# Loading eight 128 x 128 matrices in long runs and sorting their rows on the chip, in a kernel that streams 128 products

## The chip, the cores and the metric

The kernel runs on one core of a Trainium2 chip. The metric is the device time of one execution in microseconds (us); smaller is better. The kernel before takes 323.64 us (median of three runs, 323.44 to 323.72). Engines have short names in the profile: PE (TensorE), DVE (VectorE), ACT (ScalarE), POOL (GpSimd), SP (SyncE). ScalarE and SyncE each issue DMA transfers into a queue of their own; the transfers of both run on the core's 16 DMA engines.

## The reference

All of it is in float32. `x` holds 128 matrices of 128 x 1024, `weights` eight matrices of 128 x 128, and `itok_B_0_7` names for each x one of the eight (0 to 7). What is computed is x plus the product with the chosen matrix:

```
w = weights[subjects]                        # (128, 128, 128): b, c, d
out = x + einsum('bct,bcd->bdt', x, w)       # (128, 128, 1024)
```

x and the output are 67.1 MB each, the eight matrices 0.52 MB.

## The kernel before

The work goes in 32 turns of four x (`H * G` = 4, `NT` = 32), each turn in two halves of two. The x of a turn live in one of 12 slots of `x_all` (16 KB in each partition); turn i uses slot i mod 12. A slot is loaded, its products are added in place, and it is stored from the same place.

Each engine has its own list of work, written out by hand in one critical section; semaphores tie the lists together:

- **ScalarE** only issues loads (lines 200 to 204): four for a turn, each of one x (512 KB) by `transfer` (line 59), with the DRAM side written as 32 runs of 16 KB (`ROWS` = 4 rows of x in a run). The first 12 turns wait for nothing; from turn 12 on it waits until the slot's last store has landed (`s_slot`, line 202).
- **SyncE** issues the subjects (line 180) and then the matrices (line 181). The matrices go to `w_all[c, s, d]`, partition c: with `weights.rearrange("s c d -> c s d")` each contiguous run is one row of 128 elements, 512 B, so there are 1024 runs. Then it waits until slot 7 has been loaded (line 213, `AHEAD` = 8), and from there it stores turn after turn, each as soon as its additions are counted in `s_added` (lines 214 to 218; the last turn in halves, the very last x by line 238).
- **GpSimd** only waits for the loads of each turn and then raises `s_ready` (lines 206 to 211).
- **VectorE** clears a tile for PE's idle products (line 183), puts the subjects in order (193 to 199), waits for the matrices (line 222), copies the first four chosen matrices to `ws` (`place`, line 153) and then loops over the turns: for each half it adds the product from PSUM to x in place (`add`, line 174) and copies the next turn's two matrices.
- **TensorE** runs three idle products on zeros (line 186), then loops over the turns: for each half it waits for `s_go` (matrices in `ws`) and `s_ready` (x loaded), and does four products of 128 x 128 by 128 x 512 (line 162).

So the order of the transfers is set by two lists: loads in ScalarE's, stores in SyncE's. Whatever stands ahead of a load in ScalarE's list delays that load and all behind it.

Of the kernel before, what the change touches and what calls it, by code (L numbers as in the profile page):

```python
# [30 lines left out]
G = 2  # L31
H = 2
# [3 lines left out]
SLOTS = 12  # L36
# [5 lines left out]
DMA = 16  # L42

IDLE = 3

ROWS = 4

ALIGN = 4096
QUEUES = {mybir.EngineType.SP: "qSPDynamicHW", mybir.EngineType.Activation: "qActDynamicHW"}
# [2 lines left out]
def transfer(nc, engine, out, in_):  # L52

    later, nc._always_lower_symbolic_ap = nc._always_lower_symbolic_ap, False
    ins, outs = engine.lower_ap_dma(in_), engine.lower_ap_dma(out)
    nc._always_lower_symbolic_ap = later
    return engine.add_instruction(
        mybir.InstDMACopy(  # L60
            name=nc.get_next_instruction_name(),
            engine=engine.engine,
            ins=ins,
            outs=outs,
            mode="Copy",
            cce_op=ALU.bypass,
            queue=QUEUES[engine.engine],
        )
    )
# [3 lines left out]
def kernel(  # L73
# [7 lines left out]
    nc = tc.nc  # L81
    B, C, T = x.shape
    S, _, D = weights.shape
    NT = B // (G * H)

    def sbuf(name, *shape, dtype=F32):
        return ctx.enter_context(nc.sbuf_tensor(name, list(shape), dtype)).ap()
# [5 lines left out]
    x_all = sbuf("x_all", C, SLOTS * H * G * T)  # L93
# [1 line left out]
        x_all[:, i * H * G * T : (i + 1) * H * G * T].rearrange("c (q t) -> c q t", t=T)  # L95
        for i in range(SLOTS)
    ]
    w_all = sbuf("w_all", C, S, D)
    ws = [sbuf(f"w{i}", C, 1, D) for i in range(H * G)]
    zeros = sbuf("zeros", C, N)  # L100
    given, near, wrap = (sbuf(name, 1, B, dtype=I32) for name in ("given", "near", "wrap"))
# [3 lines left out]
    ]  # L105

    s_given = tc.alloc_semaphore("s_given")
    s_wall = tc.alloc_semaphore("s_wall")
    s_index = tc.alloc_semaphore("s_index")
    s_zeros = tc.alloc_semaphore("s_zeros")  # L110
# [9 lines left out]
    def emptied(i):  # L120
        turns = i // SLOTS
        return DMA * (H * G + 1) * turns - (DMA * G if i >= SLOTS and i % SLOTS == 0 else 0)

    def load(engine, i, q):
        transfer(
            nc,
            engine,
            xs[i % SLOTS][:, q, :],
            x[i * H * G + q].rearrange("(a r) t -> a (r t)", r=ROWS),
        ).then_inc(s_head if i * H * G + q < G else s_slot[i % SLOTS], DMA)  # L130

    def store(i, q0, q1):
        b = i * H * G
        transfer(
            nc,
            nc.sync,
            out[b + q0 : b + q1].rearrange("g d t -> d g t"),
            xs[i % SLOTS][:, q0:q1, :].rearrange("d (o g) t -> d o (g t)", g=min(G, q1 - q0)),
        ).then_inc(s_slot[i % SLOTS], DMA)

    def subjects_of(i):
        _, subject = nc.values_load_multi_w_load_instructions(
            index[0:1, i] if isinstance(i, slice) else index[0:1, bass.ds(i * (H * G), H * G)],
            engines=[mybir.EngineType.DVE],
            min_val=0,
            max_val=S - 1,
            skip_runtime_bounds_check_because="the index is clamped on the chip above",
        )
        return subject

    def place(h, subject):
        for q in range(h * G, (h + 1) * G):
            copy = nc.vector.tensor_copy(ws[q], w_all[:, bass.ds(subject[q], 1), :])  # L153
        copy.then_inc(s_go, 1)

    def multiply(slot, h):
        nc.tensor.wait_ge(s_go, 1).then_inc(s_go, -1)
        nc.tensor.wait_ge(s_ready, 1).then_inc(s_ready, -1)  # L158
        for q in range(h * G, (h + 1) * G):
            for t in range(0, T, N):  # L160
                at = slot * (H * G * T) + (q * T + t)
                mm = nc.tensor.matmul(  # L162
                    ps[h][:, q % G, t : t + N],
                    ws[q][:, 0, :],
                    x_all[:, bass.ds(at, N)],
                    start=True,
                    stop=True,
                )
        mm.then_inc(s_product, 1)

    def add(slot, h):
        mine = x_all[:, bass.ds(slot * (H * G * T) + h * G * T, G * T)]
        nc.vector.wait_ge(s_product, 1).then_inc(s_product, -1)  # L173
        nc.vector.tensor_tensor(  # L174
            mine, ps[h].rearrange("d g t -> d (g t)"), mine, ALU.add
        ).then_inc(s_added, 1)

    with tc.tile_critical():  # L178

        nc.sync.dma_start(given, subjects.rearrange("(o b) -> o b", o=1)).then_inc(s_given, DMA)  # L180
        nc.sync.dma_start(w_all, weights.rearrange("s c d -> c s d")).then_inc(s_wall, DMA)

        nc.vector.memset(zeros, 0.0).then_inc(s_zeros, 1)  # L183
        nc.tensor.wait_ge(s_zeros, 1)
        for _ in range(IDLE):
            nc.tensor.matmul(  # L186
                ps[P_SLOTS - 1][:, G - 1, :N], zeros[:, :D], zeros, start=True, stop=True
            )

        nc.vector.memset(index[:, B:], 0).then_inc(s_index, 1)  # L193
        nc.vector.wait_ge(s_given, DMA)
        nc.vector.tensor_scalar(near, given, -S, S - 1, ALU.max, ALU.min).then_inc(s_index, 1)  # L195
        nc.vector.wait_ge(s_index, 2)
        nc.vector.tensor_scalar(wrap, near, 0, S, ALU.is_lt, ALU.mult).then_inc(s_index, 1)  # L197
        nc.vector.wait_ge(s_index, 3)
        nc.vector.tensor_tensor(index[:, :B], near, wrap, ALU.add).then_inc(s_index, 1)  # L199
        for i in range(NT):  # L200
            if i >= SLOTS:
                nc.scalar.wait_ge(s_slot[i % SLOTS], emptied(i))
            for q in range(H * G):
                load(nc.scalar, i, q)

        for i in range(NT):
            if i == 0:
                nc.gpsimd.wait_ge(s_head, DMA * G).then_inc(s_ready, 1)
                nc.gpsimd.wait_ge(s_slot[0], DMA * G).then_inc(s_ready, 1)
            else:  # L210
                nc.gpsimd.wait_ge(s_slot[i % SLOTS], emptied(i) + DMA * H * G).then_inc(s_ready, H)

        nc.sync.wait_ge(s_slot[AHEAD - 1], DMA * H * G)
        for i in range(NT):
            for h in range(H):
                if i == NT - 1 or h == H - 1:
                    nc.sync.wait_ge(s_added, i * H + h + 1)
                    store(i, h * G if i == NT - 1 else 0, (h + 1) * G - (i * H + h == NT * H - 1))


        nc.vector.wait_ge(s_index, 4)
        nc.vector.wait_ge(s_wall, DMA)
        subject = subjects_of(slice(0, H * G))
        for h in range(H):
            place(h, subject)
        with nc.vector.Fori(0, NT) as turn:  # L226
            subject = subjects_of(turn + 1)
            for h in range(H):
                add(turn % SLOTS, h)
                place(h, subject)  # L230
        with nc.tensor.Fori(0, NT) as turn:
            for h in range(H):
                multiply(turn % SLOTS, h)
# [39 lines left out]
```

## Time and profile before

| | us |
|---|---|
| median of three runs (lowest, highest) | 323.64 (323.44, 323.72) |
| the profiled execution | 323.44 |
| its span, first to last instruction | 321.7 |
| PE busy | 244.1 |
| DVE busy | 165.7 |
| POOL busy | 0.2 |

The span is what the trace covers; the rest of the execution's time, 1.74 us, lies around it. ScalarE has no row of busy time, since it only issues transfers, which do not count as busy.

How to read the lines that the prediction quotes. A page divides the span into 40 equal slices; in the row `DMA` each digit is the mean busy share of the 16 DMA engines in tenths, in `GB/s` what they moved. A queue's line has its packets, its MB and the time of its packets as a share of 16 engines' time. A line of the view by stretches begins with the stretch (from:to, us), then its length, then each engine's busy time and instructions (PE, PE's weight loads, DVE, POOL), then the granted PE clock, the share of the DMA engines (packets overlap a little, so it can pass 1) and GB/s. A line of a group has busy time in us, mean ns of one, and the idle time before the group with what ended it. A line of the timeline begins with start and length in us. `ACTq` and `SPq` are the transfers' issues on ScalarE's and SyncE's lists; in a view of one line they have least, median and longest issue in ns, and the first and the last start.

### The profile page before, as it was taken

Reading aid. Unit: us, or ns where it says so; the run is one execution under the profiler, and the core shown is the slowest. Engines: PE = TensorE matmul, PEld = TensorE weight load, DVE = VectorE, ACT = ScalarE, POOL = GpSimd, SP = SyncE. Lnnn points to the kernel's source line nnn. Section 1 sums busy time; section 2 is a strip of 40 time slices with the busy share of each in tenths; the row PEclk is TensorE's granted clock in tenths of the full one; section 3 lists DMA queues with packets and bytes.
Section 4 is the critical chain, followed back from the end, with each engine's and each line's share of the span. In section 5 each row is a group of like instructions: output and inputs, shape, how many; then the busy total and the mean of one; then the engine's idle time right before and its main releaser. Section 6 shows DMA issues by size and latency. Waiting matters only on the chain. (4 is left out here: it accounts for less than half of the span.)

```text
span 321.7 us, 2380 instructions
## 1 busy us (share of the span) xinstructions
PE 244.1 (76%) x518; PEld 101.0 (31%) x518; DVE 165.7 (52%) x202; POOL 0.2 (0%) x4
## 2 busy tenths in 40 slices
PE   5999999999999999959499684986959779300000
PEld 2434444443444444424143231432423234000000
DVE  2267776777677677736627465371754707500000
POOL 0000000000000000000000000000000000000000
PEclk9799999999999999979879999897998959755555
DMA  7999999999999999999999999999999999999997
GB/s 281 426 428 426 424 424 408 421 437 418 421 438 428 422 418 426 439 427 423 424 418 425 434 435 413 426 433 427 428 418 425 440 417 421 426 430 425 427 428 309
DMA packets 16051, 134.76 MB, mean 419 GB/s; under 512 B 2609, under 2 KB 3634, under 8 KB 3890
## 3 DMA queue, kind: packets, MB, share of 16 engines
q1 hardware_dynamic: 9906, 67.64, 50.1%
q10 hardware_dynamic: 6144, 67.12, 49.6%
q14 instruction: 1, 0.01, 0.0%
HBM read 67.63 MB, written 67.11 MB: 419 GB/s over the span
## 5 line engine op out<-in xcount | busy, mean ns | idle before, releaser
L162 PE MATMUL ps<-x_all,w 128*128 x512 | 239.6, 626 | 30.2 <-PEq L158 27.1
L174 DVE TENSOR_TENSOR x_all<-ps,x_all 128x2048 f32 x64 | 146.7, 2292 | 106.9 <-DVEq L173 106.9
L162 PEld LDWEIGHTS ps<-x_all,w 128*128 128x128 f32 x512 | 99.3, 199 | 170.5 <-issue 169.7
L153 DVE COPY w<-w_all 128x128 f32 x132 | 23.2, 219 | 4.3 <-DMA w_all<-in_L_cond_weights_dram 4.3
L186 PE MATMUL ps<-zeros 128*128 128x512 f32 x6 | 4.4, 897 | 1.7 <-DVE zeros L183 1.7
L186 PEld LDWEIGHTS ps<-zeros 128*128 128x128 f32 x6 | 1.7, 304 | 3.6 <-issue 1.9
L183 DVE MEMSET zeros<- 128x512 f32 x1 | 0.5, 485 | 1.0 <-SPq L178 1.0
L195 DVE TENSOR_SCALAR near<-given 1x128 int32<-1x128 int32 x1 | 0.2, 217 | 0.6 <-DMA given<-in_itok_B_dram 0.6
L199 DVE CUSTOM_DVE_ANT_0 index<-near,wrap 1x256 uint16<-1x256 uint16 x1 | 0.3, 280 | 0.0
L197 DVE TENSOR_SCALAR wrap<-near 1x128 int32<-1x128 int32 x1 | 0.2, 215 | 0.0
L260 POOL MEMSET const-bfloat16-1.0<- 128x1 bf16 x1 | 0.1, 101 | 0.0
L260 POOL MEMSET const-uint8-127<- 128x1 uint8 x1 | 0.1, 101 | 0.0
L260 POOL MEMSET const-float32-0.0<- 128x1 f32 x1 | 0.1, 98 | 0.2 <-issue 0.2
L260 POOL MEMSET const-float32-1.0<- 128x1 f32 x1 | 0.1, 98 | 0.0
L260 DVE BASE_LOAD x1 | 0.0, 21 | 0.1
L193 DVE MEMSET index<- 1x4 int32 x1 | 0.1, 62 | 0.0
## 6 DMA issues: line engine op xcount, KB each, us to landing
x_all<-in_x_dram ACTq DMA_DIRECT2D x128, 512.0 KB, 10.7
out_dram<-x_all SPq DMA_DIRECT2D x31, 2048.0 KB, 54.8
out_dram<-x_all SPq DMA_DIRECT2D x1, 1024.0 KB, 26.0
out_dram<-x_all SPq DMA_DIRECT2D x2, 512.0 KB, 21.0
w_all<-in_L_cond_weights_dram SPq DMA_DIRECT2D x1, 512.0 KB, 5.1
given<-in_itok_B_dram SPq DMA_DIRECT2D x1, 0.5 KB
```

The costliest lines, as they stand in the source:

```text
L153: copy = nc.vector.tensor_copy(ws[q], w_all[:, bass.ds(subject[q], 1), :])
L162: mm = nc.tensor.matmul(ps[h][:, q % G, t : t + N], ws[q][:, 0, :], x_all[:, bass.ds(at, N)], start=True, stop=True,)
L174: nc.vector.tensor_tensor(mine, ps[h].rearrange("d g t -> d (g t)"), mine, ALU.add).then_inc(s_added, 1)
L183: nc.vector.memset(zeros, 0.0).then_inc(s_zeros, 1)
L186: nc.tensor.matmul(ps[P_SLOTS - 1][:, G - 1, :N], zeros[:, :D], zeros, start=True, stop=True)
L193: nc.vector.memset(index[:, B:], 0).then_inc(s_index, 1)
L195: nc.vector.tensor_scalar(near, given, -S, S - 1, ALU.max, ALU.min).then_inc(s_index, 1)
L197: nc.vector.tensor_scalar(wrap, near, 0, S, ALU.is_lt, ALU.mult).then_inc(s_index, 1)
L199: nc.vector.tensor_tensor(index[:, :B], near, wrap, ALU.add).then_inc(s_index, 1)
L260: nc = _bacc.Bacc("TRN2", target_bir_lowering=False, num_devices=1)
```

## The change

The matrices are read in the order in which they lie in DRAM, by the same helper and in the same form as an x: 32 runs of 16 KB. They land in `w_runs`, where partition p holds eight rows, those of matrix s = p // 16 with c from 8 (p mod 16) on; but a product needs c as the partition. Three steps bring the rows there:

1. VectorE transposes `w_runs` in blocks of 32 x 32 into `w_turned` (one instruction, 128 x 1024).
2. ScalarE makes 16 copies of 32 partitions x 256 elements from `w_turned` to `w_moved`: one for each pair of a source and a destination group of 32 partitions. They take rows of eight elements 128 elements apart and write them side by side.
3. VectorE transposes `w_moved` back into `w_runs`, which is now `w_all` in the old arrangement.

`w_turned` and `w_moved` lie in slot 11 of `x_all`, and so turn 11's loads wait for the second transposition. ScalarE's copies stand in its list behind the loads of turns 0 to 5 (`EARLY` = 6), after a wait for the first transposition. VectorE's second transposition waits for all 16 copies, and `place` for that.

```diff
+EARLY = 6
+
+BLOCK = 32
...
-    w_all = sbuf("w_all", C, S, D)
+
+    RUN = S
+    PER = BLOCK * RUN // C
+    BLOCKS = C // BLOCK
+    w_runs = sbuf("w_runs", C, S * D)
+    w_all = w_runs.rearrange("c (s d) -> c s d", s=S)
+
+    spare = x_all[:, (SLOTS - 1) * H * G * T :]
+    w_turned, w_moved = (spare[:, i * S * D : (i + 1) * S * D] for i in range(2))
...
+    s_moved = tc.alloc_semaphore("s_moved")
...
-        nc.sync.dma_start(w_all, weights.rearrange("s c d -> c s d")).then_inc(s_wall, DMA)
+
+        transfer(
+            nc,
+            nc.sync,
+            w_runs,
+            weights.rearrange("s c d -> (s c d)").rearrange("(a r) -> a r", r=ROWS * T),
+        ).then_inc(s_wall, DMA)
...
         for i in range(NT):
+            if i == EARLY:
+                nc.scalar.wait_ge(s_wall, DMA + 1)
+                for a in range(BLOCKS):
+                    for b in range(BLOCKS):
+                        nc.scalar.copy(
+                            w_moved[b * BLOCK : (b + 1) * BLOCK, :].rearrange(
+                                "l (a m h k j) -> l a h m k j", a=BLOCKS, m=PER, j=RUN, k=BLOCK // RUN
+                            )[:, a],
+                            w_turned[a * BLOCK : (a + 1) * BLOCK, :].rearrange(
+                                "l (j h m b k) -> l b h m k j", j=RUN, m=PER, b=BLOCKS, k=BLOCK // RUN
+                            )[:, b],
+                        ).then_inc(s_moved, 1)
+            if i == SLOTS - 1:
+                nc.scalar.wait_ge(s_wall, DMA + 2)
             if i >= SLOTS:
                 nc.scalar.wait_ge(s_slot[i % SLOTS], emptied(i))
...
         nc.vector.wait_ge(s_index, 4)
         nc.vector.wait_ge(s_wall, DMA)
+
+
+
+
+        nc.vector.transpose(w_turned, w_runs).then_inc(s_wall, 1)
+        nc.vector.wait_ge(s_moved, BLOCKS**2)
+        nc.vector.transpose(w_runs, w_moved).then_inc(s_wall, 1)
+        nc.vector.wait_ge(s_wall, DMA + 2)
         subject = subjects_of(slice(0, H * G))
```

## The prediction

> **What bounds the kernel now.** I read the page first: its 40 slices, then its DMA queues. The page of before has:
>
> ```profile
> span 321.7 us, 2380 instructions
> ...
> DMA  7999999999999999999999999999999999999997
> GB/s 281 426 428 426 424 424 408 421 437 418 421 438 428 422 418 426 439 427 423 424 418 425 434 435 413 426 433 427 428 418 425 440 417 421 426 430 425 427 428 309
> ...
> q1 hardware_dynamic: 9906, 67.64, 50.1%
> q10 hardware_dynamic: 6144, 67.12, 49.6%
> ```
>
> The reader is to see that the 16 DMA engines are full in every slice but the first and the last: SyncE's queue (q1: stores, matrices, subjects) and ScalarE's (q10: the x loads) fill 99.7% of the span between them. PE's and DVE's shares do not matter as long as the DMA engines have work. The view by stretches gives the rate (last column GB/s, before it the share of the DMA engines):
>
> ```profile
> 12.00:44.00 32.00, 32.00 (x74) 13.44 (x73) 22.27 (x25) 0.00 (x0) 1.00 1.01 426
> ...
> 100.00:200.00 100.00, 83.90 (x182) 34.60 (x180) 60.17 (x72) 0.00 (x0) 0.95 1.01 426
> 200.00:260.00 60.00, 48.12 (x97) 19.93 (x98) 30.72 (x36) 0.00 (x0) 0.90 1.01 426
> 260.00:318.00 58.00, 15.91 (x32) 6.32 (x30) 10.24 (x12) 0.00 (x0) 0.62 1.01 426
> ```
>
> Loads alone (12 to 44 us), loads and stores mixed, and stores alone (PE does little after 260 us) all run at 426 GB/s. So the time is a start, plus bytes divided by 0.426 MB/us, plus whatever is lost to slow packets or to engines without work. The change keeps the bytes, so it can act in two places: the matrices' own packets near the start, and idle time of the DMA engines if loads or stores come too late. The last view is the timeline of the first 35 us:
>
> ```profile
> 0.90 34.21 ACTq L59 DMA_DIRECT2D x_all<-in_x_dram  x39
> ...
> 1.36 0.42 SPq L181 DMA_DIRECT2D w_all<-in_L_cond_weights_dram  x1
> ...
> 7.31 0.63 DVE L153 COPY w<-w_all 128x128 f32 x4 [4.31 <-DMA w_all<-in_L_cond_weights_dram]
> ...
> 8.30 26.98 PE L162 MATMUL ps<-x_all,w 128*128 x57 [2.21 <-PEq L158]
> ...
> 17.36 2.29 DVE L174 TENSOR_TENSOR x_all<-ps,x_all 128x2048 f32 x1 [0.81 <-DVEq L173]
> ...
> 24.42 2.29 DVE L174 TENSOR_TENSOR x_all<-ps,x_all 128x2048 f32 x1 [0.81 <-DVEq L173]
> ```
>
> PE's first product starts at 8.30 us, turn 0 (four matrices of x) is added by 17.36 + 2.29 = 19.65 us, and a turn takes 24.42 - 17.36 = 7.06 us. Yet nothing is stored until 44.8 us, when slot 7 has landed (the wait in line 213):
>
> ```profile
> L59 SPq DMA_DIRECT2D out_dram<-x_all x6: 611/774/9635, 44.8 to 55.0; - x6
> ```
>
> **The gain: the matrices' packets.** Two views of the DMA queues, of 4.0 to 5.4 us and of 0 to 8 us:
>
> ```profile
> DMA packets 919, 0.47 MB, mean 334 GB/s; under 512 B 7, under 2 KB 919, under 8 KB 919
> ...
> q1 hardware_dynamic: 912, 0.47, 110.4%
> q10 hardware_dynamic: 7, 0.00, 0.3%
> ```
>
> ```profile
> q1 hardware_dynamic: 1042, 0.52, 22.0%
> ```
>
> From 4.0 to 5.4 us the engines carry the 512-byte runs of the matrices alone, with no gap, at 334 GB/s. All of the matrices are 8 x 128 x 128 x 4 B = 0.524 MB: 0.524 / 0.334 = 1.57 us. In runs of 16 KB they are exactly one more load of x (x[b] is also 0.524 MB in 32 runs of 16 KB), which takes 0.524 / 0.426 = 1.23 us. **The gain is 0.34 us.** From above it is bound by packet time: 22.0% of 8 us is 1.76 us of each engine, against 49.6% of 321.7 us / 128 = 1.25 us for a load of x, so 0.51 us; from below by nothing.
>
> [...]
>
> **The cost: what could leave the DMA engines idle.** ScalarE is the engine that issues all loads of x. Its 16 copies and the wait ahead of them now stand before load 24 (i = 6), and every later load is queued behind them. Its issues until 16.5 us, and after, with first and last start:
>
> ```profile
> L59 ACTq DMA_DIRECT2D x_all<-in_x_dram x24: 533/617/708, 0.9 to 15.8; - x24
> ```
>
> ```profile
> L59 ACTq DMA_DIRECT2D x_all<-in_x_dram x23: 891/1050/2422, 16.5 to 43.9; - x23
> ```
>
> ```profile
> 0.00:16.50 16.50, 12.64 (x21) 5.30 (x22) 4.36 (x13) 0.20 (x4) 0.90 0.89 354
> ```
>
> ScalarE issues far faster (0.62 us) than the engines move (1.23 us). At 16.5 us it has issued 24 x 0.524 + 0.52 = 13.1 MB, of which 0.354 x 16.5 = 5.8 MB have moved; 7.3 MB are still queued, which is 17.1 us of work. From an issue to its first packet it takes 1.3 us: ScalarE's first issue starts at 0.90 us and the first busy tenth of a microsecond is the 23rd, at 2.2 us, in the view of 0 to 4 us:
>
> ```profile
> DMA  0000000000000000000000999940000949940003
> ```
>
> So ScalarE may be away for 17.1 - 1.3 = **15.8 us** before an engine runs dry: 0.98 us for each of 16 copies. How long is a copy (32 partitions, 256 elements in rows of 8)? No ScalarE instruction stands in the trace. Nearest rows of the page:
>
> ```profile
> L174 DVE TENSOR_TENSOR x_all<-ps,x_all 128x2048 f32 x64 | 146.7, 2292 | 106.9 <-DVEq L173 106.9
> ...
> L153 DVE COPY w<-w_all 128x128 f32 x132 | 23.2, 219 | 4.3 <-DMA w_all<-in_L_cond_weights_dram 4.3
> ...
> L193 DVE MEMSET index<- 1x4 int32 x1 | 0.1, 62 | 0.0
> ```
>
> A plain instruction costs 219 ns at 128 elements and 2292 at 2048, that is 1.08 ns an element: 256 elements take 219 + 128 x 1.08 = 357 ns, and 16 copies 5.7 us. From below, 16 x 62 ns = 1.0 us. From above, if each of the 32 rows of 8 cost as much as the smallest instruction, 32 x 62 ns = 1.98 us, and 16 copies 31.7 us. I take 5.7 us, because the copy's size lies between those of the first two rows; then the loads queued hide the copies nearly three times over, and they cost nothing.
>
> [...]
>
> The other steps, each on its queue:
> - The first transposition (128 x 1024) waits for the matrices, which land 5.1 us after their issue at 1.36 us:
>
> ```profile
> w_all<-in_L_cond_weights_dram SPq DMA_DIRECT2D x1, 512.0 KB, 5.1
> ```
>
>   It costs between 219 + 896 x 1.08 = 1.2 us and, at a 128 x 128 copy for each 128 columns, 8 x 219 ns = 1.75 us; I take 1.5. It is done near 8 us, long before ScalarE comes to its wait at 16.5 us; even 10 us of it would hold nobody.
> - The second one ends at 16.5 + 5.7 + 1.5 = 23.7 us. Behind it on DVE stand all copies of matrices and all additions, and PE waits for those. PE's first product followed the landing of the matrices at 6.5 us by 1.8 us; it now starts at about **25.5 us instead of 8.3**. The cover is line 213: turn 0 is added 19.65 - 8.30 = 11.4 us after the first product, at 36.9 us, still before the first store may go at 44.8 us. From there a turn comes every 7.06 us, while its 2.1 MB in and 2.1 MB out keep the DMA engines busy for 4.19 / 0.426 = 9.8 us: products get ahead of stores again, the store queue does not run dry, and the order of the transfers stays that of before. If that cover went (first product after 33.4 us), stores would begin later, and the loads up to slot 11, 48 x 1.23 = 59 us of work, would still fill the engines.
> - At the end PE has 32 turns x 7.06 = 226 us of work from 25.5 us, so it could be through at 252 us. Its last product now comes after 260 us (row 260:318 above, 32 of its products), held by loads, and after it the engines still have over 40 us of stores. Nothing of the late start is left there.
> - The load of slot 11, where the turned matrices lie, waits for the second transposition; ScalarE comes to it 20 loads after the copies. At 0.62 us each that is past 16.5 + 5.7 + 12.4 = 34.6 us, and the transposition is done at 23.7. It costs nothing.
> - SyncE issues the matrices in some 0.6 us instead of 0.42; its next issue is at 44.8 us. POOL has no new work.
>
> **Sum.** The profiled execution took 323.44 us (1.74 us around its span of 321.7) and becomes 323.44 - 0.34 = 323.10. The median of the three runs shown lies 0.20 higher, at 323.64. I forecast 323.64 - 0.34 = **323.3 us**. 0.2% of it, about what a measurement of this kernel can tell from no change, is 0.65 us: this is within it.
>
> **Rivals.**
> 1. *No gain*: 323.6. At the start, runs of 16 KB may be no faster than the small ones. For: in the row below the very first load goes at 297 GB/s, slower than the matrices. Against: from 12 us on such runs go at 426. Chance 0.08.
>
> ```profile
> 2.20:4.00 1.80, 1.80 (x3) 0.67 (x2) 0.71 (x3) 0.00 (x0) 1.00 0.94 297
> ```
>
> 2. *The ramp goes too*: from 2.2 to 4.0 us, 1.8 x (426 - 297) / 426 = 0.55 us are lost. If that comes of building 1024 small runs beside load 0, it goes with them: 323.64 - 0.34 - 0.55 = 322.75, faster by 0.28%. For: load 1, issued at about 1.5 us, moves only after the matrices. Against: any first packet may be slow. Chance 0.16.
> 3. *ScalarE starts later*: something that its first copy needs is set up ahead of its first load. The matrices, issued at 1.36 us, then go first, at 1.36 + 1.3 = 2.66 us, until 3.9: a delay of up to 1.7 us costs 2.66 - 2.2 = 0.46 us (323.8), and one as long as the longest issue in the row above, 2.42 us, brings the first load to 4.62 us and costs 0.46 + 0.72 = 1.18 us (**324.5**, slower). For: no ScalarE instruction runs before the change. Against: the copies stand behind 24 loads in its order. Chance 0.12, half of it slower.
> 4. *The copies outlast the queue* (slower). Decides from 0.98 us a copy, at the place where ScalarE should issue load 24. Price: all beyond 15.8 us; at the upper bound 31.7 - 15.8 = 15.9 us, **339.2**. For: rows of 8 elements with a large step, unlike anything in the trace. Against: 0.98 us is 2.7 times the estimate. Chance 0.10.
>
> That the change does not do what it says (the matrices' runs being cut to 4 KB, one for each partition) falls under the forecast or rival 1: x's loads have the same shape on both sides, and q10's 6144 packets are 128 x (32 + 16), 32 of them runs of 16 KB and 16 signals.
>
> **How the numbers follow.** Forecast 0.54, rival 1 0.08, rival 2 0.16, rival 3 0.12, rival 4 0.10. Faster by over 0.2%: rival 2, 0.16. Slower: rival 4 and half of rival 3, 0.16. Within: 0.68. The range takes in rival 2, the packet bound (323.13), rival 1 and rival 3 nearly to its upper price: 322.7 to 324.4. Outside are rival 4 and the tail of rival 3, about 0.15.
>
> **What would show it.** Right: q1's share in the first 8 us falls from 22.0% to about 15.6% (1.25 of 8 us); no stretch between 4 and 44 us under 420 GB/s; the first product near 25 us; the first store still at about 44.5 us; 426 GB/s to the end. Wrong: a hole in the DMA slices around 33 us (rival 4); ScalarE's first issue after 0.90 us (rival 3); over 400 GB/s between 2.2 and 4 us (rival 2). And the whole argument is wrong if the engines run dry after 45 us because the additions come late.

## The result: slower by 0.15%, and the profile after

The changed kernel takes **323.98 us** (median of 22 runs, 323.64 to 324.74); the kernel before, run on the same chips, 323.50 (22 runs, 323.16 to 323.83). The ratio is 1.0015 with a 95% interval of 1.0009 to 1.0021: slower by about half a microsecond, small, but outside what the measurement leaves open. The forecast was 0.34 us faster. The profiled execution of after took 323.93 us at a span of 322.2.

The page of after has the rows that the prediction began with:

```profile
span 322.2 us, 2399 instructions
...
DMA  7999999999999999999999999999999999999996
GB/s 291 425 423 427 429 410 410 438 420 419 431 432 428 417 422 425 430 423 425 429 423 426 427 431 422 424 429 436 427 411 425 437 415 427 426 425 426 426 429 279
...
q1 hardware_dynamic: 8914, 67.64, 49.9%
q10 hardware_dynamic: 6144, 67.12, 49.6%
```

q1 has 992 packets fewer (1024 runs became 32), and they take 49.9% of 322.2 us instead of 50.1% of 321.7, which is 0.4 us less of each DMA engine. Yet the span is longer by 0.5 us, and there is no hole: all slices but the first and the last are full, as before. By this page nothing is lost, and the time is longer.

The matrices do move faster. The queue's row for 0 to 8 us (22.0% before), and the row of the issue (5.1 us before):

```profile
q1 hardware_dynamic: 50, 0.52, 17.5%
```

```profile
w_runs<-in_L_cond_weights_dram SPq DMA_DIRECT2D x1, 512.0 KB, 4.4
```

The sorting, from the page's costliest groups (busy time, ns of one, idle time before it and what ended it):

```profile
L262 DVE STREAM_TRANSPOSE w_runs<-x_all 128x1024 f32<-128x1024 f32 x1 | 1.2, 1245 | 21.0 <-ACT x_all L224 21.0
L224 ACT COPY x_all<-x_all 32x256 f32<-32x256 f32 x16 | 9.8, 614 | 0.4
...
L260 DVE STREAM_TRANSPOSE x_all<-w_runs 128x1024 f32<-128x1024 f32 x1 | 1.2, 1245 | 2.8 <-DMA w_runs<-in_L_cond_weights_dram 2.8
L224 ACT ACT_TABLE_LOAD x1 | 1.3, 1283 | 16.6 <-issue 16.6
```

VectorE waits 21.0 us for ScalarE's copies. The timelines of after for ScalarE, VectorE, PE and SyncE (start and length in us):

```profile
0.90 15.64 ACTq L63 DMA_DIRECT2D x_all<-in_x_dram  x24
16.57 1.28 ACT L224 ACT_TABLE_LOAD   x1 [16.57 <-issue]
17.87 7.64 ACT L224 COPY x_all<-x_all 32x256 f32<-32x256 f32 x12
24.91 1.12 ACTq L63 DMA_DIRECT2D x_all<-in_x_dram  x2
```

```profile
28.09 1.25 DVE L262 STREAM_TRANSPOSE w_runs<-x_all 128x1024 f32<-128x1024 f32 x1 [21.00 <-ACT x_all L224]
30.10 0.63 DVE L166 COPY w<-w_runs 128x128 f32 x4 [0.77 <-DVE w_runs L262]
```

```profile
31.01 14.17 PE L175 MATMUL ps<-x_all,w 128*128 x26 [24.63 <-DVE w L166]
```

```profile
44.08 0.69 SPq L63 DMA_DIRECT2D out_dram<-x_all  x1
```

ScalarE issues no load from 16.54 to 24.91 us; PE's first product moves from 8.30 to 31.01; the first store still goes at 44.08. So the plan held: the products start 23 us late, and the stores do not.

Where does the time go, then? Two groups of stretches answer (in each line, last two columns: share of the DMA engines, GB/s). First before, then after:

```profile
2.20:44.00 41.80, 39.59 (x84) 16.34 (x83) 23.61 (x32) 0.00 (x0) 0.96 1.01 419
44.00:52.00 8.00, 8.00 (x20) 3.22 (x18) 5.89 (x9) 0.00 (x0) 1.00 1.01 408
52.00:318.00 266.00, 195.94 (x417) 80.98 (x416) 135.71 (x159) 0.00 (x0) 0.87 1.01 426
319.00:319.40 0.40, 0.00 (x0) 0.00 (x0) 0.00 (x0) 0.00 (x0) 0.50 1.00 410
319.40:319.80 0.40, 0.00 (x0) 0.00 (x0) 0.00 (x0) 0.00 (x0) 0.50 0.44 174
319.80:320.20 0.40, 0.00 (x0) 0.00 (x0) 0.00 (x0) 0.00 (x0) 0.50 0.10 41
320.20:320.60 0.40, 0.00 (x0) 0.00 (x0) 0.00 (x0) 0.00 (x0) 0.50 0.00 0
```

```profile
2.20:44.00 41.80, 17.17 (x30) 6.67 (x29) 8.96 (x15) 11.10 (x17) 0.00 (x0) 0.67 1.01 422
44.00:52.00 8.00, 8.00 (x19) 3.49 (x19) 5.43 (x7) 0.00 (x0) 0.00 (x0) 1.00 1.01 397
52.00:318.00 266.00, 213.82 (x471) 88.74 (x469) 153.32 (x180) 0.00 (x0) 0.00 (x0) 0.90 1.01 426
319.00:319.40 0.40, 0.00 (x0) 0.00 (x0) 0.00 (x0) 0.00 (x0) 0.00 (x0) 0.50 0.90 369
319.40:319.80 0.40, 0.00 (x0) 0.00 (x0) 0.00 (x0) 0.00 (x0) 0.00 (x0) 0.50 0.24 92
319.80:320.20 0.40, 0.00 (x0) 0.00 (x0) 0.00 (x0) 0.00 (x0) 0.00 (x0) 0.50 0.07 31
320.20:320.60 0.40, 0.00 (x0) 0.00 (x0) 0.00 (x0) 0.00 (x0) 0.00 (x0) 0.50 0.07 31
```

Three things are to be seen.

1. *The gain is there at 44 us.* 41.8 us at 422 instead of 419 GB/s is 0.125 MB more, worth 0.125 / 0.426 = 0.29 us.
2. *Most of it is given back in the next 8 us*, where the first stores come in beside the loads: 397 against 408 GB/s is 8 x 11 / 426 = 0.21 us. From 52 to 318 us both run at 426.
3. *The end is uneven.* From 319.0 to 319.8 us after moves less than before (most of its engines are already done), but then goes on until past 320.6 at a share of 0.07, about 1/16: **one engine of the 16 works alone** while the others have finished. Before is through by 320.2, but for a last packet.

The view of the transfers from 319.8 to 320.8 us shows this one engine (its first row has the share in 40 slices):

```profile
DMA  3000003000000300000300000300000300000000
...
DMA packets 7, 0.02 MB, mean 25 GB/s; under 512 B 1, under 2 KB 1, under 8 KB 7
```

Six packets of 4 KB, 0.16 us apart, and a signal of 4 B: a single engine's last pieces, one after the other.

How far is it behind the others? The trace has each packet's start, length, size and queue, but not its engine. Of the 15134 packets of before that start between 5 and 318 us, 15125 do so 3 to 4 ns before the end of another (14778 of 14789 in after); with that one taken for the packet ahead on the same engine, the packets can be strung into 16 rows. Worked out so (the engine that ends last, against the median engine, in us of work; and the end of each):

```
           lag of the last engine at                 median engine's  last engine's  execution
           100    150    200    250    300 us        last signal      last packet    us
before     0.03   0.26   0.39   0.58   0.70          319.59           320.28         323.44
after      0.08   0.31   0.71   1.06   1.24          319.53           320.76         323.93
```

The median engine ends at the same time (319.59, 319.53). The last one ends 0.48 us later, and the execution is 0.49 us longer: it ends 3.16 and 3.17 us after that engine's last packet. The lag grows over 200 us, by a few ns a packet: from about 90 us on (with a handful earlier), single packets of that one engine take 313 to 354 ns where its other stores of 8 KB take 309 to 312, or 618 to 652 where its loads take 611 to 617. The other 15 have next to none of these. A share of 16 engines cannot show it: 0.5 us of one engine in 266 us is 0.01%.

### The profile page after: what moved, and what is told of

The parts are those of the page before. It is cut to its first block, busy times and chain, and to the rows that moved or that the text cites. A ratio compares the mean times of both kernels' runs of the same rounds, so it can differ in the third digit from the quotient of the medians.

```text
span 322.2 us, 2399 instructions
## 1 busy us (share of the span) xinstructions
PE 239.5 (74%) x518; PEld 99.4 (31%) x518; DVE 168.2 (52%) x204; ACT 11.1 (3%) x17; POOL 0.2 (0%) x4
## 3 DMA queue, kind: packets, MB, share of 16 engines
q1 hardware_dynamic: 8914, 67.64, 49.9%
## 5 line engine op out<-in xcount | busy, mean ns | idle before, releaser
L175 PE MATMUL ps<-x_all,w 128*128 x512 | 234.8, 617 | 35.2 <-DVE w L166 24.6
L187 DVE TENSOR_TENSOR x_all<-ps,x_all 128x2048 f32 x64 | 146.7, 2292 | 84.6 <-DVEq L186 84.6
L175 PEld LDWEIGHTS ps<-x_all,w 128*128 128x128 f32 x512 | 97.6, 196 | 172.4 <-issue 171.5
L166 DVE COPY w<-w_runs 128x128 f32 x132 | 23.2, 219 | 0.8 <-DVE w_runs L262 0.8
L262 DVE STREAM_TRANSPOSE w_runs<-x_all 128x1024 f32<-128x1024 f32 x1 | 1.2, 1245 | 21.0 <-ACT x_all L224 21.0
L224 ACT COPY x_all<-x_all 32x256 f32<-32x256 f32 x16 | 9.8, 614 | 0.4
L260 DVE STREAM_TRANSPOSE x_all<-w_runs 128x1024 f32<-128x1024 f32 x1 | 1.2, 1245 | 2.8 <-DMA w_runs<-in_L_cond_weights_dram 2.8
L224 ACT ACT_TABLE_LOAD x1 | 1.3, 1283 | 16.6 <-issue 16.6
```

The lines of the kernel that those rows point to most:

```text
L175: mm = nc.tensor.matmul(ps[h][:, q % G, t : t + N], ws[q][:, 0, :], x_all[:, bass.ds(at, N)], start=True, stop=True,)
L187: nc.vector.tensor_tensor(mine, ps[h].rearrange("d g t -> d (g t)"), mine, ALU.add).then_inc(s_added, 1)
L224: nc.scalar.copy(w_moved[b * BLOCK : (b + 1) * BLOCK, :].rearrange("l (a m h k j) -> l a h m k j", a=BLOCKS, m=PER, j=RUN, k=BLOCK // RUN) ...
L260: nc.vector.transpose(w_turned, w_runs).then_inc(s_wall, 1)
L262: nc.vector.transpose(w_runs, w_moved).then_inc(s_wall, 1)
```

## The experiments

Three causes were possible for the loss: that PE's products start late; the long runs themselves; ScalarE's copies and its pause in issuing loads. The expectations call them by letters, and each says what it would mean for the time. The first four kernels and the one before ran on one chip (before: 323.56, 33 runs; each of the four 11 runs).

**Runs alone (e1).** The changed kernel without the 16 copies, the transpositions and their waits.

```diff
-            if i == EARLY:
...
-        nc.vector.transpose(w_turned, w_runs).then_inc(s_wall, 1)
-        nc.vector.wait_ge(s_moved, BLOCKS**2)
-        nc.vector.transpose(w_runs, w_moved).then_inc(s_wall, 1)
-        nc.vector.wait_ge(s_wall, DMA + 2)
```

> Only the first part of the change: the matrices come in 16 KB runs, and nothing sorts them (no transpositions, no copies, so the products use rows in the wrong order). First product near 8 us as before. Theory L (the late start of the products costs it: stores are handed out one at a time and one DMA engine ends behind the others): 323.2, that is 0.2 to 0.34 us under before (323.5), with the last engine at most 0.7 us behind the median one at the end. Theory W (the long runs themselves put an engine behind): 324.0, like the changed kernel. Theory C (ScalarE's pause in issuing loads does it): 323.2.

Measured: 323.63, ratio 1.0003 (0.9994 to 1.0012). No theory gave this time (323.2 or 324.0): the runs alone neither gain nor cost what can be measured. Their two stretches:

```profile
2.20:44.00 41.80, 40.77 (x87) 16.42 (x86) 24.54 (x35) 0.00 (x0) 1.00 1.01 423
44.00:52.00 8.00, 8.00 (x19) 3.33 (x18) 6.03 (x7) 0.00 (x0) 1.00 0.99 374
```

Ahead at 44 us by 41.8 x 4 / 426 = 0.39 us, behind by 8 x 34 / 426 = 0.64 in the next 8 us.

**Late, without long runs (e2).** The matrices in 512-byte runs as before, the sorting done on the side, and VectorE waits for it. ScalarE's copies stay in (11.10 us of it busy between 2.2 and 44 us, as in after), and with them its pause; so this run takes out the long runs only, and does not part the late start from the pause.

```diff
-        transfer(
-            nc,
-            nc.sync,
-            w_runs,
...
+        nc.sync.dma_start(w_all, weights.rearrange("s c d -> c s d")).then_inc(s_wall, DMA)
...
-        nc.vector.transpose(w_runs, w_moved).then_inc(s_wall, 1)
+        nc.vector.transpose(w_side, w_moved).then_inc(s_wall, 1)
```

> Only the second part: the matrices come in 512-byte runs straight into their place as before, and the two transpositions and 16 copies work on the side, on scratch, but VectorE still waits for them before the first product. First product near 32 us. Theory L: 0.5 to 0.8 us over before, 324.0 to 324.3. Theory W: 323.5, no change. Theory C: 324.0 to 324.3.

Measured: 323.84, 1.0008 (0.9999 to 1.0017); the first product at 31.0 us. Its value lies toward that of after, under the 324.0 to 324.3 of theories L and C, and its interval just holds 1.

**Copies beside (e3).** The long runs, the first transposition and ScalarE's copies stay; VectorE goes on at once, so the first product is at 7.9 us.

```diff
-                nc.scalar.wait_ge(s_wall, DMA + 2)
+                nc.scalar.wait_ge(s_moved, BLOCKS**2)
...
-        nc.vector.wait_ge(s_moved, BLOCKS**2)
-        nc.vector.transpose(w_runs, w_moved).then_inc(s_wall, 1)
-        nc.vector.wait_ge(s_wall, DMA + 2)
```

> The changed kernel, but VectorE does not wait for ScalarE's copies (the second transposition is left out, so the products use rows in the wrong order): ScalarE pauses for its 16 copies as in the changed kernel, the first product comes near 8 us. Theory L: 323.2. Theory W: 324.0. Theory C: 324.0.

Measured: 323.76, 1.0009 (1.0000 to 1.0018). This touches 1 and lies between the 323.2 of theory L and the 324.0 of W and C: taken alone it settles nothing about the pause.

**Stores later (e4).** The changed kernel, with the first store after slot 9 instead of 7.

```diff
-AHEAD = 8
+AHEAD = 10
```

> The changed kernel with the first store held until slot 9 has landed (AHEAD = 10), near 53 us, when two turns are added instead of one. Theory L in its narrow form (it is the first stores, handed out one at a time from 44 us, that put an engine behind): under 323.8. Theory L in its wide form (stores handed out every 7 us until products have caught up with loads, near 200 us), W and C: 324.0, no change against the changed kernel.

Measured: 324.00, 1.0012 (1.0003 to 1.0021), as after; theory L in its narrow form falls. Letting the additions get further ahead of the stores brings nothing back.

Of the second four, three take the kernel before and change one thing each, and the fourth builds on the kernel with runs alone (before: 323.48, 27 runs; the first three 11 runs each, the fourth one run).

**Only a wait (g1).** The products of before wait for slot 7; runs, copies and transpositions are not in it.

```diff
         nc.vector.wait_ge(s_wall, DMA)
+        nc.vector.wait_ge(s_slot[AHEAD - 1], DMA * H * G)
```

> The kernel before (512-byte runs, no transpositions, no copies) with one wait more: VectorE waits for slot 7 ahead of its first copies, so the first product comes near 46 us. Theory P (while PE works, from about 90 us on, the packets of one DMA engine are slowed a little; the more of PE's work lies there, the later that engine ends, and the time is its end): 324.0 to 324.2, the last engine 1.2 us or more behind the median one. Theory S (stores handed out one at a time put an engine behind): 323.9 or more. Theory C (it needs ScalarE's copies): 323.6, like before.

Measured: **324.01**, 1.0022 (1.0012 to 1.0032). The first product is at 46.35 us and ScalarE issues as before. So a late start by itself makes this kernel slower, with no long runs and no pause of ScalarE's; it is the only run that has a late start alone, and the start is 15 us later than that of after. Its end is that of after, one engine alone from 319.8 on:

```profile
319.80:320.20 0.40, 0.00 (x0) 0.00 (x0) 0.00 (x0) 0.00 (x0) 0.50 0.05 20
320.20:320.60 0.40, 0.00 (x0) 0.00 (x0) 0.00 (x0) 0.00 (x0) 0.50 0.07 31
```

**More products (g2).** One product in four is done twice; the start is as before.

```diff
-            for t in range(0, T, N):
+            for t in ([0] if q % G == 0 else []) + list(range(0, T, N)):
```

> The kernel before with one product in four done twice (into the same place, so the output is the same): PE needs some 8.8 us for a turn instead of 7.06, starts at 8.3 us as before, but hardly waits any more until 276 us. Theory P: 323.9 to 324.2, the last engine about 1.2 us behind. Theories S and C: 323.6.

Measured: 323.68, 1.0008 (0.9999 to 1.0017): leaning to slower, with an interval that just holds 1. Theory P's 323.9 to 324.2 is missed; in the profiled execution (323.95) the last engine does end 1.20 us behind the median one.

**Stores held (g3).** Each store of before waits for three more turns, so that stores are not handed out one by one as the additions end.

```diff
-                    nc.sync.wait_ge(s_added, i * H + h + 1)
+                    nc.sync.wait_ge(s_added, min((i + 3) * H + h + 1, NT * H) if i < NT - 1 else i * H + h + 1)
```

> The kernel before, but each store waits until three more turns are added: the products start at 8.3 us, the stores are handed out one at a time, every 7 us from 44.8 us, as in the changed kernel. Theory P: 323.6, like before. Theory S: 323.9 or more.

Measured: 323.43, 0.9999 (0.9990 to 1.0008). Handing the stores over later makes no difference that can be measured; the theory of the stores falls.

**Small runs too (g4).** The kernel with runs alone, and the matrices a second time in 512-byte runs, into slot 11, whose loads wait for them.

```diff
+        nc.sync.dma_start(
+            spare[:, : S * D].rearrange("c (s d) -> c s d", s=S), weights.rearrange("s c d -> c s d")
+        ).then_inc(s_moved, DMA)
...
+                nc.scalar.wait_ge(s_moved, DMA)
```

> As the run with 16 KB runs alone (no sorting, so the products use rows in the wrong order), but a second transfer brings the same matrices once more in 512-byte runs into the unused slot 11, right behind. Only for the loads beside the first stores: 20 to 26 of them are slow in the kernels with 512-byte runs, 39 to 41 in those without. If it is the small runs in SyncE's queue that make the difference: about 20 to 26 here; if not, about 40. The time is not of interest (1.5 us more of transfers).

One run: 324.85, with 0.52 MB more to move (0.52 / 0.426 = 1.2 us). What counts is the first stores. Beside them some loads' packets of 16 KB take 0.7 to 1.3 us instead of 0.61; counted over all engines after 40 us, and their excess for each engine:

```
                 runs in SyncE's queue     slow packets   excess, us
before           512 B                     20             0.41
e2, g2, g3       512 B                     26, 26, 34     0.39, 0.46, 0.43
g4               16 KB and 512 B           18             0.26
after            16 KB                     40             0.58
e1, e3, e4       16 KB                     39, 41, 40     0.83, 0.68, 0.74
h3, h4           16 KB                     38, 39         0.47, 0.62
```

With the small runs in the queue it is 18 to 34 of them, without 38 to 41. (g1 is left out, since its stores begin at 58 us.) Adding the small runs back halves the count in one execution, which speaks for the small runs but does not show it; and the excess does not part the two groups (0.46 in g2, 0.47 in h3).

What remained was the growing lag of one engine. Do its slow packets come while PE or VectorE work? They end in before at 276.3 us, PE's last product at 275.9; in the kernel with more products at 285.4 and 284.9. The last four kernels test that. In the two with a tail the last store (line 238) waits for the tail, so **their own times mean nothing**; only the packets of 280 to 318 us do.

**A tail on PE (h1).** Behind the last addition 64 idle products on zeros.

```diff
+        nc.tensor.wait_ge(s_added, NT * H)
+        with nc.tensor.Fori(0, 16):
+            for _ in range(4):
+                nc.tensor.matmul(ps[0][:, 0, :N], zeros[:, :D], zeros, start=True, stop=True)
```

> The kernel before, and behind the last addition PE does 64 idle products on zeros, some 38 us, while only stores run. In the runs so far the last slowed packet comes within 3 us of PE's last product. If PE's running alone slows the packets of one engine: slowed store packets until near 314 us and an end 0.2 to 0.3 us later (323.7 to 323.8). If it takes the turns' own work (loads, additions, copies of matrices): none after 280 us, 323.5.

The time is 342.15 (1.0504, 1.0462 to 1.0547). **A tail on VectorE (h2)**, 96 small copies, each awaited:

```diff
+        with nc.vector.Fori(0, 24):
+            for _ in range(4):
+                nc.vector.tensor_copy(side, ps[1][:, 0, : N // 2]).then_inc(s_side, 1)
+                nc.vector.wait_ge(s_side, 1).then_inc(s_side, -1)
```

> The kernel before, and behind its loop VectorE makes 96 small copies out of PSUM, each with a semaphore, some 40 us, while only stores run. If VectorE's running (or its semaphores) slows the packets: slowed store packets until near 315 us and 323.7 to 323.8. If it is PE: none after 280 us, 323.5.

The time is 345.02 (1.0657, 1.0640 to 1.0673). The stretch of 280 to 318 us, of before, of the tail on PE and of that on VectorE (PE, its weight loads, VectorE, GpSimd):

```profile
280.00:318.00 38.00, 0.00 (x0) 0.00 (x0) 0.00 (x0) 0.00 (x0) 0.50 1.01 425
```

```profile
280.00:318.00 38.00, 37.41 (x84) 16.60 (x85) 0.73 (x3) 0.00 (x0) 0.96 1.01 426
```

```profile
280.00:318.00 38.00, 0.00 (x0) 0.00 (x0) 25.68 (x63) 0.00 (x0) 0.53 1.01 425
```

The rate of all engines is the same (425, 426). But the slow packets of the one engine, which stop in before, go on: till 317.6 us with PE busy, till 317.5 with VectorE alone busy. Their excess by stretch, in us:

```
          90-130  130-170  170-210  210-250  250-280  280-320
before    0.31    0.13     0.15     0.13     0.10     0.00
after     0.32    0.28     0.28     0.29     0.16     0.00
h1 (PE)   0.26    0.09     0.09     0.17     0.12     0.17
h2 (DVE)  0.17    0.11     0.19     0.15     0.14     0.21
```

So in these runs they come while PE or VectorE executes instructions, and stop when neither does (0.17 and 0.21 us after 280 us with a tail, 0.00 without); it takes neither the turns' products nor their additions. After differs from before mostly between 130 and 250 us. The stretch of 130 to 210 us, of before and of after:

```profile
130.00:210.00 80.00, 63.90 (x133) 26.58 (x133) 42.24 (x49) 0.00 (x0) 0.91 1.01 426
```

```profile
130.00:210.00 80.00, 80.00 (x182) 33.23 (x180) 58.24 (x69) 0.00 (x0) 0.00 (x0) 1.00 1.01 426
```

Before has caught up with its loads by then and waits for them; after, which began 23 us late, still works through its backlog, with 182 products instead of 133.

**Both again (h3 and h4).** The changed kernel and the one with runs alone, unchanged, on the chip of the two tails.

> The changed kernel once more, on the same chip as the next one. All theories: 0.4 to 0.6 us over before, 323.9 to 324.1; last engine 1.0 us or more behind the median one.

> The run with 16 KB runs alone once more (no sorting, rows in the wrong order), beside the changed kernel. If its early products are what keeps it fast: within 0.15 us of before, 0.3 us or more under the changed kernel, slowed packets adding up to some 0.8 us in its profile instead of the 1.16 of the first time.

Measured: 323.90, 1.0011 (1.0002 to 1.0020), and 323.63, 1.0003 (0.9994 to 1.0012). Both repeat, though 0.27 us apart where 0.3 or more was expected. None of the twelve is faster than the kernel before by what can be measured.

The profiled executions in order of time, with the sum of the slow packets after 90 us:

```
             us       sum, us   first product at
before       323.44   0.82       8.3
e3           323.52   0.78       7.9  (0.24 below its own median)
g3           323.55   0.82       8.0
h4           323.59   0.78       7.6
h3           323.65   1.00      31.3
e2           323.79   1.25      31.0
g1           323.87   1.19      46.4
after        323.93   1.32      31.0
g2           323.95   1.19       8.3  (more products)
e1           324.05   1.16       8.0  (0.42 above its own median)
e4           324.23   1.35      31.2
```

Time and sum go together through the eleven, if not strictly (g4, which moves more bytes, and the tails are left out). Strung into rows in the same way, all eleven have their median engine through between 319.49 and 319.74 us, and the last one 0.69 to 1.40 us later, which is the kernel's sum to within 0.14 us; each execution ends 3.16 to 3.18 us after that engine's last packet. So it is the slow packets that tell these executions apart. The sum is 0.78 to 0.82 in four of the five kernels with an early start and as many products as before, 1.00 to 1.35 in the others. The rows of e1 and e3 are a fair warning: they are the slowest and the fastest execution of their kernels, and a kernel with an early start can have a sum of 1.16 too.

## Why the prediction was wrong, point by point

**The step that failed** is the one at the end: "Nothing of the late start is left there", and with it the whole sum 323.64 - 0.34, which carried a gain at the start through to the end. The sum treated the 16 engines as one pool of 426 GB/s. The pool's rate was right (426 from 52 to 318 us, no hole), but of the gain the median engine shows only 0.06 us at its end (319.53 against 319.59). And the time is that of the last engine, which gathers its delay while PE and VectorE work: 1.24 us instead of 0.70. The late start, for which the prediction reckoned nothing, costs 0.53 us where it stands alone (g1, 324.01 against 323.48). That it does so by moving work into the time in which the delay grows (182 - 133, some 50 products, between 130 and 210 us) fits the traces and is argued, not shown.

Point by point:

- *The matrices' packets.* Right in direction: 22.0% of 8 us became 17.5%, 1.76 us to 1.40 (forecast 15.6%, 1.25). The gain forecast at 0.34 us was 0.29 at 44 us by the rows above.
- *The gain reaches the end.* Wrong: 0.21 us are given back in 44 to 52 us, where the prediction saw no cost. With runs alone nothing measurable is left (1.0003).
- *The copies lie beside the queued loads.* Right as far as no DMA engine ran dry, with a size off. A copy takes 614 ns, not 357, and a table load of 1283 ns comes ahead of them. ScalarE was away for 24.91 - 16.54 = 8.4 us of the 15.8 that were free, and 12 to 44 us went at 426 GB/s (second row below; the first belongs to rival 2). The first copy starts 1.30 us after the load does (17.87 - 16.57).

```profile
2.20:4.00 1.80, 1.80 (x3) 0.68 (x2) 0.71 (x3) 0.00 (x0) 0.00 (x0) 1.00 1.26 428
...
12.00:44.00 32.00, 12.99 (x24) 5.35 (x25) 7.00 (x11) 11.10 (x17) 0.00 (x0) 0.62 1.01 426
```

- *The transpositions.* 1245 ns each; taken as 1.5 us, lower bound 1.2.
- *The first product.* Forecast 25.5 us, measured 31.0: the copies (+4.1 us), the table load (+1.3). The cover still held (the first store at 44.08), and no rival about it came true.
- *Rival 1* (no gain, 323.6) named the time of runs alone, but not its reason. *Rivals 3 and 4* did not happen: ScalarE's first issue is still at 0.90 us, and there is no hole near 33 us. *Rival 2* did not either: 0.55 us more would have shown at 44 us. The row of 2.2 to 4.0 us reads 428 GB/s after the change, the sign that the prediction named for it, but at a share of 1.26, which no set of engines can have; a packet's bytes are put to where it starts, and so the stretch is too short for packets of 0.6 us. No rival had a late start that costs time with full DMA engines.

**What is shown, what is argued, what is open.** Shown: a late start alone costs time (g1, first product at 46 us); the runs alone bring none (e1, h4); in the profiled executions the last engine sets the end, and its lag grows packet by packet while PE or VectorE execute (h1, h2). Argued: that in the changed kernel, with its start at 31 us, it is the late start and not ScalarE's pause (e2 has both, e3 the pause alone, and neither is clear of no change); and that the number of instructions after 90 us sets how far the lag grows. It fits in direction (332 products between 90 and 318 us and 0.82 us in before, 385 and 1.32 in after), but is not proportional (418 and 1.19 in g1), and the kernel with more products gave no clear time. Open: what on that one engine is disturbed, why this begins near 90 us, whether and how the small runs of the matrices thin out the slow packets at the first stores, and whether ScalarE's pause adds anything (e3). Nor does any run tell whether the recording of the profile itself disturbs that engine: every execution here has a span and a granted clock, so each was recorded, and a trace holds records of PE's and VectorE's instructions.

## What to carry to other kernels

When transfers fill the span, compute the end from the last DMA engine and not from the mean of the 16: here the median engines of the two kernels ended 0.06 us apart, the last ones 0.48. Look at the last microsecond in slices of 0.4 us: the share of 0.07 there, about 1/16, was one engine working alone. Hidden compute was not free here: work put off until later still ran beside transfers, and cost 0.53 us of 323.48 in the run that does nothing else (g1). A gain of some tenths of a microsecond at the start of a long stream has to be followed to the end before it is counted: of the 0.29 us at 44 us here, 0.21 were given back by 52 us, where the first stores came in.

## What the runs showed of the hardware that was not expected

- In the packets strung into rows, one DMA engine of the 16, and but for single packets only one, had packets 2 to 43 ns longer while PE or VectorE executed instructions, from about 90 us on: 96 of them and 0.82 us in before, 142 and 1.32 us in after. From 280 us on, with stores alone, it had none in before and after, and 0.17 and 0.21 us with a tail on PE (h1) or on VectorE (h2).
- At the first stores single 16 KB packets of loads took 0.7 to 1.3 us instead of 0.61: 18 to 34 of them in the five kernels with 512-byte runs in SyncE's queue (before, e2, g2, g3, g4), 38 to 41 in the six without (after, e1, e3, e4, h3, h4).
- A ScalarE copy of 32 x 256 elements with rows of eight took 614 ns. One table load of 1283 ns stood ahead of the first copy, at 16.57 us, and none at the start of the program.
- A 32 x 32-block transposition of 128 x 1024 float32 on VectorE took 1245 ns, 5% more than the estimate from the rows of a copy (219 ns at 128 elements) and an addition (2292 ns at 2048): 219 + 896 x 1.08 = 1187 ns.
